# Preparing the maps of attention and of the experts between the feed-forward's slots, and splitting the first map's weights after the first gates

## The chip, the cores and the metric

The kernel runs on one core of one Trainium2 chip. The metric is the device time of one execution in microseconds (us), the lower the better; several executions are timed and their median is taken. A profiled execution gives for every instruction its engine, start and duration. The engines are PE (matrix multiplication; PEld are its weight loads), DVE (vector), ACT (activation), POOL (general) and SP, which here only issues DMAs. "Lnnn" in a line of the profile is a line of the kernel; L83 is a helper through which most operations pass.

## The reference

The input is x [4, 128, 64, 64], float32. Four layers follow, cut here to what the change touches:

```python
x = x + L0_conv_ref(gn(x))                    # layer 0: deformable convolution
x = g * x + x                                 # layer 1 ends with a gate g = sigmoid(conv(o) + b)
t = to_tokens(x)                              # [4, 4096, 128]

# layer 2, first half: products of cosines, then a feed-forward over 8 of 128 channels
def L2_attn_ref(x):
    a = x.reshape(B, S, 16, 8) + theta
    cp = cumprod(cos(a), axis=-1)
    x1 = layernorm(x + concat([cp[..., -1:], cp[..., 1:]]), gamma1, beta1)
    q = cos(phi) * cos(x1[..., :8])
    h = relu(q @ w1.T + b1)                   # 8 -> 2048
    return layernorm(x1 + h @ w2.T + b2, gamma2, beta2)
t = t + L2_attn_ref(ln(t))

# layer 2, second half, and layer 3, second half: eight experts, the best two of each token
def ffn_ref(x):
    p = softmax(x @ router_w + router_b); top_p, top_i = top_k(p, 2)
    e = einsum('bnd,edc->bnec', x, expert_w) + expert_b
    return sum over the two of top_p / sum(top_p) * e[top_i]
t = t + ffn_ref(ln(t))

# layer 3, first half: additive attention over the earlier tokens
def L3_attn_ref(x):
    f, g = x @ W1[:128], x @ W1[128:]         # 16 columns each
    score = tanh(f_i + g_j + b1) @ w2 + b2
    e = exp(score) * (j < i)
    return (e / (e.sum(j) + 1e-10)) @ x
t = t + L3_attn_ref(ln(t))
t = t + ffn_ref(ln(t))
```

## The kernel before

The whole activation stays in on-chip memory as one tile X of 128 partitions by 16,384 columns. The function at the end of the file calls the layers in turn: layer0, layer1, layer2, attention_maps, then for the experts of layer 2 moe_prepare and moe, then moe_prepare for layer 3, attention, and moe again.

**Order.** Most operations go through an object InOrder: each is pinned behind the one traced before it on the same engine. Operations issued with the plain engine object may be placed elsewhere on their engine by the scheduler. Memory is taken from pools that are opened and closed around a stage; PSUM, where PE writes, is handed out in tiles of 512 columns.

**layer2** works on 16 groups (p) of eight tiles of 128 tokens. It first loads the feed-forward's first weights by 16 DMAs on SP (L1522) and splits them into a leading and a remaining part with eight instructions (L1526 iota on POOL, to L1532 on DVE). The gates of layer 1 come next: gate(k) loads a block `oin` by SP, multiplies on PE into `psg`, takes the sigmoid on ACT into `g`, updates X on DVE, and two steps later transposes X on PE (`psf`) and copies it back on ACT. Four gates run ahead; the others stand between the slots of the first groups.

A loop over p from -3 to 16 and s from 0 to 7 calls slot(p, s). One slot issues on PE four matmuls `phh` of the next half group's hidden units (32 rows each, one buffer each, of a pool of four), then four matmuls for each of two sums `pff`, and between them the other stages of groups p+3 (A: first normalization, u, turns k, remainder a), p+2 (cosine, products on POOL in a_products, B: second normalization), p+1 and p-1 (D: third normalization; ptt transposes back, d_add adds it to x1, d_norm on ACT, d_sum with three POOL instructions adds to X). Of the four phh of a slot, DVE rectifies one or none (ON_VECTOR) and ACT the others into `hid`. The gates' psg and psf use the same four buffers (tag "phh").

**attention_maps** (L2056 to L2139) works out the small matrices of attention's approximation, hide, wf, wg, cw, sb, sw and tiny, from W1, w2 and the biases: three loads, an iota and shifts, some 30 small DVE instructions, transposes and matmuls through a PSUM tile `aux`.

**moe_load** and **moe_prepare** load the router and expert weights (`rw`, `ew`), subtract their last row from all rows (two matmuls by `last` into `pse`, L1834, and one into `psw`, L1838; the subtractions are L1836 and L1839), replace the last row by the biases with two DMAs on SP (L1840, L1841), clear `rws` (L1842) and copy the router's weights into it four times (L1844). moe then starts with an iota, `rank`, and the statistics of its first tiles (bn_stats into `w`).

**attention** starts with a memset of the eight tiles `v` on POOL, then statistics(0, 0): bn_stats of eight tiles into `st`, variance with seven POOL instructions, the root on ACT, the normalization into `v`, transposes `D`, the copy `vT`, and the factors F and G. SP writes X to memory (`kept`, L2161) at its start.

Of the kernel before, what the change touches and what calls it, by code (L numbers as in the profile page):

```python
# [27 lines left out]
NE = 8  # L28
# [61 lines left out]
class Kernel:  # L90
# [1400 lines left out]
    def layer2(self):  # L1491
# [8 lines left out]
        with ExitStack() as ctx:  # L1500
# [24 lines left out]
            nc.gpsimd.iota(half, pattern=[[0, 1]], base=0, channel_multiplier=1)  # L1525
            nc.vector.tensor_scalar(half, half, 4, 1, ALU.arith_shift_right, ALU.bitwise_and)  # L1526
            nc.vector.tensor_copy(parts[:, 1:2], half)
            nc.vector.tensor_scalar(parts[:, 0:1], parts[:, 1:2], -1.0, 1.0, ALU.mult, ALU.add)
            nc.vector.tensor_copy(w1b.bitcast(F32R), w1a)
            nc.vector.tensor_sub(w1a, w1a, w1b)  # L1530
            nc.vector.tensor_scalar(w1b, w1b, parts[:, 0:1], None, ALU.mult)
            nc.vector.scalar_tensor_tensor(w1T, w1a, parts[:, 1:2], w1b, ALU.mult, ALU.add)  # L1532
# [7 lines left out]
            V, S, G = nc.vector, nc.scalar, nc.gpsimd  # L1540

# [270 lines left out]
    def moe_load(self, ctx, layer):  # L1812
        cp = ctx.enter_context(self.tc.tile_pool(name=f"m{layer}w", bufs=1, side="right" if layer == 2 else None))
        rw = self.load(cp, f"router_w{layer}", [P, NE], eng=self.nc.sync)
        ew = self.load(cp, f"expert_w{layer}", [P, NE * P], eng=self.nc.sync)
        self.moe_maps[layer] = rw, ew

    def moe_prepare(self, ctx, layer):


        tc, nc = self.tc, self.nc
        LAST = P - 1
        rw, ew = self.moe_maps[layer]

        cp = ctx.enter_context(tc.tile_pool(name=f"m{layer}r", bufs=1))
        rws = cp.tile([P, 4, P], F32, name="rws")
        self.moe_maps[layer] = ew, rws
        with tc.tile_pool(name=f"m{layer}i", bufs=1) as ip, \
                tc.tile_pool(name=f"m{layer}j", bufs=1, space=PSUM) as pp:
            last = ip.tile([P, P], F32, name="last")  # L1830
            nc.vector.tensor_copy(last, self.ident[:, LAST:P].to_broadcast([P, P]))
            ps = pp.tile([P, NE * P], F32, name="pse")
            for h in range(2):
                nc.tensor.matmul(ps[:, 512 * h:512 * (h + 1)], last, ew[:, 512 * h:512 * (h + 1)],  # L1834
                                 start=True, stop=True)
            nc.vector.tensor_sub(ew, ew, ps)  # L1836
            ps = pp.tile([P, NE], F32, name="psw")
            nc.tensor.matmul(ps, last, rw, start=True, stop=True)  # L1838
            nc.vector.tensor_sub(rw, rw, ps)  # L1839
            nc.sync.dma_start(ew[LAST:P, :], self.ins[f"expert_b{layer}"].rearrange("e c -> (e c)").unsqueeze(0))  # L1840
            nc.sync.dma_start(rw[LAST:P, :], self.ins["rows"][ROW[f"router_b{layer}"]].unsqueeze(0))  # L1841
            nc.vector.memset(rws, 0.0)  # L1842
            for j in range(4):
                nc.vector.tensor_copy(rws[:, j, 32 * j:32 * j + NE], rw)  # L1844
# [211 lines left out]
    def attention_maps(self, ctx):  # L2056


        tc, nc = self.tc, self.nc
        LAST = P - 1  # L2060
        cp = ctx.enter_context(tc.tile_pool(name="r3k", bufs=1))
        with tc.tile_pool(name="r3a", bufs=2, space=PSUM) as aux, tc.tile_pool(name="r3w", bufs=1) as wp:
            w1f = self.load(wp, "att_w1f", [P, P])
            w1g = self.load(wp, "att_w1g", [P, P], view=self.ins["att_w1g"][:, 0, :])
            w2z = self.load(wp, "att_w2z", [P, 56])
            hide = cp.tile([P, P], F32, name="hide")
            nc.gpsimd.memset(hide, 0.0)
            nc.gpsimd.affine_select(out=hide, in_=hide, compare_op=ALU.is_gt, fill=1.0e4, base=0,
                                    pattern=[[1, P]], channel_multiplier=-1)
            wf = [cp.tile([P, P], F32, name=f"wf{b}") for b in range(2)]  # L2070
            wg = [cp.tile([P, P], F32, name=f"wg{b}") for b in range(2)]
            cw = [cp.tile([P, 1], F32, name=f"cw{b}") for b in range(2)]
            sb = cp.tile([P, 1], F32, name="sb")
            sw = cp.tile([P, 1], F32, name="sw")

            with tc.tile_pool(name="r3m", bufs=1) as mp:

                pi = mp.tile([P, 5], I32, name="pi")
                bits = mp.tile([P, 6], F32, name="bits")
                nc.gpsimd.iota(pi, pattern=[[0, 5]], base=0, channel_multiplier=1)  # L2080
                for k in range(5):
                    nc.vector.tensor_scalar(pi[:, k:k + 1], pi[:, k:k + 1], k, 1,
                                            ALU.arith_shift_right, ALU.bitwise_and)
                nc.vector.tensor_copy(bits[:, 0:5], pi)
                has = mp.tile([P, 2, 2, 16], F32, name="has")
                nc.vector.memset(has, 0.0)
                for b in range(2):
                    nc.vector.memset(bits[:, 5:6], float(b))
                    for hs, a0, a1 in ATT_SETS:
                        nc.vector.tensor_copy(has[hs, b, 0, a0:a1], bits[hs, 0:a1 - a0])  # L2090
                        nc.vector.tensor_scalar(has[hs, b, 1, a0:a1], bits[hs, 0:a1 - a0], -1.0, 1.0,
                                                ALU.mult, ALU.add)

                last = mp.tile([P, P], F32, name="last")
                nc.vector.tensor_copy(last, self.ident[:, LAST:P].to_broadcast([P, P]))
                wd = mp.tile([P, 2, 16], F32, name="wd")
                ps = aux.tile([P, 512], F32, name="aux")
                for k, w in enumerate((w1f, w1g)):
                    nc.tensor.matmul(ps[:, k * 16:(k + 1) * 16], last, w[:, 0:16], start=True, stop=True)
                    nc.vector.tensor_sub(wd[:, k, :], w[:, 0:16], ps[:, k * 16:(k + 1) * 16])  # L2100
                sel = mp.tile([16, 4, P], F32, name="sel")
                ps = aux.tile([P, 512], F32, name="aux")
                for k in range(4):
                    nc.tensor.transpose(ps[0:16, k * P:(k + 1) * P], has[:, k // 2, k % 2, :], self.ident)
                nc.vector.tensor_copy(sel.rearrange("p k c -> p (k c)"), ps[0:16, :])
                maps = mp.tile([16, 2, P], F32, name="maps")
                ps = aux.tile([P, 512], F32, name="aux")
                for k in range(2):
                    nc.tensor.transpose(ps[0:16, k * P:(k + 1) * P], wd[:, k, :], self.ident)
                nc.vector.tensor_copy(maps.rearrange("p k c -> p (k c)"), ps[0:16, 0:2 * P])  # L2110

                bl = mp.tile([16, P], F32, name="bl")
                nc.vector.memset(bl, 0.0)
                nc.vector.tensor_copy(bl[:, LAST:P], self.col("att_b1")[0:16, :])
                nc.vector.tensor_add(maps[:, 1, :], maps[:, 1, :], bl)

                w2 = w2z[0:16, 24:25]
                for b in range(2):
                    ps = aux.tile([P, 512], F32, name="aux")
                    for k, m in enumerate((wf, wg)):  # L2120
                        nc.tensor.matmul(ps[:, k * P:(k + 1) * P], maps[:, k, :], sel[:, 2 * b, :],
                                         start=True, stop=True)
                        nc.vector.tensor_copy(m[b], ps[:, k * P:(k + 1) * P])
                    nc.tensor.matmul(ps[:, 2 * P:2 * P + 1], sel[:, 2 * b + 1, :], w2, start=True, stop=True)
                    nc.vector.memset(cw[b], 1.0)
                    for hs in ((slice(32, 64),), (slice(32, 64), slice(64, 128)))[b]:
                        nc.vector.tensor_scalar(cw[b][hs, :], ps[hs, 2 * P:2 * P + 1], 2.0, None, ALU.mult)
# [501 lines left out]
def tile_conv_attn_hybrid(ctx: ExitStack, tc: tile.TileContext, ins: dict, out: bass.AP):  # L2629
# [10 lines left out]
    with two:  # L2640
        k.moe_prepare(two, 2)
        k.moe(2)
# [82 lines left out]
```

## Time and profile before

| what | us |
|---|---|
| median of three runs | 5165.38 |
| lowest and highest | 5161.37, 5171.79 |
| the profiled execution | 5169.17 |
| its span, first to last instruction | 5167.3 |
| granted clock of PE, mean | 0.931 |
| busy time of PE, DVE, ACT, POOL | 4526.2, 3699.5, 3592.7, 3255.3 |
| gates' first matmul psg | 1851.22 |
| first phh of the feed-forward | 1938.66 |
| end of its last pff | 2526.84 |
| first bn_stats of the experts, layer 2 | 2549.01 |
| last sum of the experts, layer 2, on X | 2867.66 |
| first bn_stats of attention | 2874.61 |

The lower six rows are points on the profiled execution's time axis, in us from the span's start. A line of the timeline reads: start, duration, engine, line of the kernel, operation, output<-input, sizes, how many follow one another, and in brackets how long the engine sat idle before it and what ended that. A line of the windows reads: stretch, its length, then busy time and number of instructions of each engine, then the clock granted to PE, the busy share of the DMA engines and the GB/s moved.

### The profile page before, as it was taken

How to read it: one execution, taken by the hardware profiler on the slowest of the kernel's cores; microseconds unless marked ns; L12 is line 12 of the kernel's file. 1: busy time of each engine (PE TensorE's matmuls, PEld its weight loads, DVE VectorE, ACT ScalarE, POOL GpSimd, SP SyncE). 2: the span in 40 equal slices, each digit the busy share in tenths (PEclk: the TensorE clock that was granted, in tenths of full speed). 3: DMA queues.
4: the chain of work that ended last, by engine and by line, in shares of the span. 5: the costliest groups of instructions: out<-in, count | busy, mean ns of one | idle time of the engine just before them, and what ended most of it. 6: DMA issues, size and time to landing. Idle time of an engine off the chain costs nothing. (4 is left out here: it accounts for less than half of the span.)

```text
span 5167.3 us, 65672 instructions
## 1 busy us (share of the span) xinstructions
PE 4526.2 (88%) x22430; PEld 2474.0 (48%) x22430; DVE 3699.5 (72%) x7376; ACT 3592.7 (70%) x5440; POOL 3255.3 (63%) x3073
## 2 busy tenths in 40 slices
PE   5776777668889959999799799999999999999798
PEld 3665666536556624444344344444444444444344
DVE  3889888768988658887477566676676666665675
ACT  3353534345565557777576699999999999999675
POOL 0627365415555525555279688888788888887488
PEclk7898988888888879999899899999999999999899
DMA  5556555300000030000000000000000000000000
GB/s 170 140 139 149 143 150 142 91 6 1 17 13 11 17 90 1 1 1 1 6 17 33 17 1 1 1 1 1 1 1 1 1 1 1 1 1 1 5 29 33
DMA packets 67239, 185.59 MB, mean 36 GB/s; under 512 B 13254, under 2 KB 16518, under 8 KB 65224
## 3 DMA queue, kind: packets, MB, share of 16 engines
q1 hardware_dynamic: 56856, 164.94, 10.9%
q0 software_dynamic: 6272, 12.86, 1.5%
q8 instruction: 181, 2.97, 0.2%
q10 hardware_dynamic: 3760, 3.43, 0.2%
q14 instruction: 170, 1.39, 0.1%
HBM read 131.83 MB, written 49.36 MB: 35 GB/s over the span
## 5 line engine op out<-in xcount | busy, mean ns | idle before, releaser
L83 POOL TENSOR_TENSOR r<-r 128x512 f32<-128x512 f32 (+1 forms) x1088 | 1348.7, 1241 | 335.8 <-DVE r L83 274.9
L83 DVE TENSOR_TENSOR r<-r,num 128x1024 f32<-128x1024 f32 (+1 forms) x1088 | 975.6, 928 | 601.9 <-PE num L83 503.6
L83 PE MATMUL D<-F,G 32*128 32x512 f32 (+3 forms) x4608 | 1145.1, 576 | 1.3 <-DVE den L83 0.9
L83 PE MATMUL num<-F,G 32*128 32x512 f32 (+3 forms) x4608 | 1057.9, 590 | 6.9 <-DVE r L83 4.0
L83 ACT ACTIVATE r<-r 128x2048 f32<-128x2048 f32 (+4 forms) x610 | 1018.5, 1679 | 52.0 <-POOL r L83 5.8
L83 ACT ACTIVATE r<-D 128x1536 f32<-128x1536 f32 (+1 forms) x544 | 763.3, 1403 | 54.4 <-PE D L83 31.4
L83 PEld LDWEIGHTS D<-F,G 32*128 32x128 f32 x4608 | 487.2, 185 | 372.9 <-issue 234.2
L83 PE MATMUL acc<-ident,pr 128*128 128x128 f32 x3200 | 449.0, 304 | 221.7 <-DVE pr L83 221.7
L83 PE MATMUL acc<-r,v 128*128 128x512 f32 (+3 forms) x1152 | 598.3, 606 | 0.7 <-ACT r L83 0.7
L83 POOL DMA_INDIRECT px<-tab,idx x196 | 385.8, 1968 | 255.9 <-DMA v<-tab 164.8
L83 PEld LDWEIGHTS acc<-ident,pr 128*128 128x128 f32 x3200 | 415.8, 159 | 261.7 <-DVE pr L83 252.8
L83 POOL TENSOR_TENSOR x<-x 128x512 f32<-128x512 f32 (+2 forms) x320 | 405.6, 1267 | 150.8 <-DVE x L83 84.6
L83 PEld LDWEIGHTS num<-F,G 32*128 32x128 f32 x4608 | 384.1, 184 | 225.9 <-issue 112.4
L83 PE MATMUL pff<-hid,w_ffn_w2T 128*128 128x512 f32 x1024 | 468.5, 601 | 0.0
L83 PE MATMUL pex<-w_expert_w,vT 128*128 128x512 f32 x1024 | 462.4, 600 | 1.6 <-DVE x L83 1.6
L83 DVE TENSOR_TENSOR pr<-v,wt 128x2560 f32<-128x2560 f32 x160 | 453.7, 2851 | 9.7 <-PE acc L83 9.7
L83 PEld LDWEIGHTS acc<-r,v 128*128 128x128 f32 x1152 | 174.3, 188 | 382.4 <-issue 186.4
L83 ACT ACTIVATE x<-pex,gate 128x128 f32<-128x128 f32 x896 | 256.6, 367 | 104.9 <-PE pex L83 77.8
L83 ACT ACTIVATE hid<-phh,cols 128x512 f32<-128x512 f32 x416 | 252.8, 688 | 68.1 <-PE phh L83 68.1
L83 PEld LDWEIGHTS pex<-w_expert_w,vT 128*128 128x128 f32 x1024 | 191.2, 193 | 216.4 <-issue 160.5
L83 PEld LDWEIGHTS pff<-hid,w_ffn_w2T 128*128 128x128 f32 x1024 | 185.3, 191 | 200.6 <-issue 200.6
L83 POOL TENSOR_TENSOR X<-X,sl 128x512 f32<-128x512 f32 x32 | 76.6, 2392 | 315.4 <-ACT sl L83 315.4
(501 smaller groups left out, 7633.6 us busy)
## 6 DMA issues: line engine op xcount, KB each, us to landing
v<-tab SPq DMA_DIRECT2D x320, 256.0 KB
oms<-omw SPq DMA_DIRECT2D x32, 432.0 KB
omr<-oms SPq DMA_DIRECT2D x32, 432.0 KB
X<-in_x_dram SPq DMA_DIRECT2D x8, 1024.0 KB
tab<-vb SPq DMA_DIRECT2D x64, 128.0 KB
o<-o SPq DMA_DIRECT2D x32, 256.0 KB
oin<-o SPq DMA_DIRECT2D x32, 256.0 KB
kept<-X SPq DMA_DIRECT2D x4, 2048.0 KB
```

Source lines behind the costliest of these rows:

```text
L83: return lambda *args, **kwargs: self.tc.keep_in_program_order(op(*args, **kwargs))
```

## The change

Five parts go together.

1. The split of the first weights leaves its place ahead of the gates. Its eight instructions become first_map(), which runs in three pieces after slots 0, 1 and 2 of p=-2, each pinned behind that slot's instructions on its engine. The 16 loads stay.
2. moe_prepare for both layers and attention_maps become generators. later_maps() chains them, and one step runs after each slot from p=1 on: 37 steps, up to slot 4 of p=5. Their PSUM tiles come from bank(), which takes one of the four buffers of phh. A step either fills a bank on PE or reads it on DVE, not both.
3. The weights' and maps' places are taken before layer2 (moe_space, attention_space), and the weights are loaded by SP after the last slot of p=-1 (moe_fetch). The biases' loads are issued by SP in steps of their own.
4. In attention, the memset of `v` moves from POOL to DVE, the two instructions for `tiny` are issued there, and the variance of the first two groups runs on DVE instead of POOL.
5. The calls of attention_maps and moe_prepare between the stages are gone.

```diff
@@ layer2
-            nc.gpsimd.iota(half, pattern=[[0, 1]], base=0, channel_multiplier=1)
-            nc.vector.tensor_scalar(half, half, 4, 1, ALU.arith_shift_right, ALU.bitwise_and)
-            nc.vector.tensor_copy(parts[:, 1:2], half)
-            nc.vector.tensor_scalar(parts[:, 0:1], parts[:, 1:2], -1.0, 1.0, ALU.mult, ALU.add)
-            nc.vector.tensor_copy(w1b.bitcast(F32R), w1a)
-            nc.vector.tensor_sub(w1a, w1a, w1b)
-            nc.vector.tensor_scalar(w1b, w1b, parts[:, 0:1], None, ALU.mult)
-            nc.vector.scalar_tensor_tensor(w1T, w1a, parts[:, 1:2], w1b, ALU.mult, ALU.add)
...
+            def first_map():
+                G.iota(half, pattern=[[0, 1]], base=0, channel_multiplier=1)
+                V.tensor_scalar(half, half, 4, 1, ALU.arith_shift_right, ALU.bitwise_and)
+                V.tensor_copy(parts[:, 1:2], half)
+                V.tensor_scalar(parts[:, 0:1], parts[:, 1:2], -1.0, 1.0, ALU.mult, ALU.add)
+                yield
+                V.tensor_copy(w1b.bitcast(F32R), w1a)
+                V.tensor_sub(w1a, w1a, w1b)
+                yield
+                V.tensor_scalar(w1b, w1b, parts[:, 0:1], None, ALU.mult)
+                V.scalar_tensor_tensor(w1T, w1a, parts[:, 1:2], w1b, ALU.mult, ALU.add)
+                yield
+
+            def later_maps():
+                def bank():
+                    return ph.tile([P, 512], F32, name="phm", tag="phh")
+                mp = ctx.enter_context(tc.tile_pool(name="l2m", bufs=1))
+                last = mp.tile([P, P], F32, name="last")
+                V.tensor_copy(last, self.ident[:, P - 1:P].to_broadcast([P, P]))
+                for layer in (2, 3):
+                    yield from self.moe_prepare(nc, layer, last, bank)
+                yield from self.attention_maps(nc, mp, last, bank)
...
+            begun, beside = first_map(), later_maps()
             for p in range(-3, NG + 1):
                 for s in range(8):
                     slot(p, s)
                     for _ in range(GATES[s] if p < -1 else LAST_GATES[s] if p < 0 else 0):
                         gate(next(steps))
+                    if p == -2:
+                        next(begun, None)
+                    if p == -1 and s == 7:
+                        for layer in (2, 3):
+                            self.moe_fetch(layer)
+                    if p >= 1:
+                        next(beside, None)
...
+    def moe_fetch(self, layer):
+        rw, ew, _ = self.moe_maps[layer]
+        self.nc.sync.dma_start(rw, self.ins[f"router_w{layer}"])
+        self.nc.sync.dma_start(ew, self.ins[f"expert_w{layer}"])
+
+    def moe_prepare(self, nc, layer, last, bank):
...
+        for h in range(2):
+            hs = slice(512 * h, 512 * (h + 1))
+            ps = bank()
+            nc.tensor.matmul(ps, last, ew[:, hs], start=True, stop=True)
+            yield
+            nc.vector.tensor_sub(ew[:, hs], ew[:, hs], ps)
+            yield
+        ps = bank()
+        nc.tensor.matmul(ps[:, 0:NE], last, rw, start=True, stop=True)
+        yield
+        nc.vector.tensor_sub(rw, rw, ps[:, 0:NE])
+        nc.vector.memset(rws, 0.0)
+        yield
+        self.nc.sync.dma_start(ew[LAST:P, :], self.ins[f"expert_b{layer}"].rearrange("e c -> (e c)").unsqueeze(0))
+        self.nc.sync.dma_start(rw[LAST:P, :], self.ins["rows"][ROW[f"router_b{layer}"]].unsqueeze(0))
+        for _ in range(3):
+            yield
+        for j in range(4):
+            nc.vector.tensor_copy(rws[:, j, 32 * j:32 * j + NE], rw)
+        yield
...
@@ attention_maps, one of its pairs of steps
+        sel = mp.tile([16, 4, P], F32, name="sel")
+        ps = bank()
+        for k in range(4):
+            nc.tensor.transpose(ps[0:16, k * P:(k + 1) * P], has[:, k // 2, k % 2, :], self.ident)
+        yield
+        nc.vector.tensor_copy(sel.rearrange("p k c -> p (k c)"), ps[0:16, :])
+        yield
...
@@ attention
-                    nc.gpsimd.memset(v[:, :, LAST:P], 1.0)
+                    nc.vector.memset(v[:, :, LAST:P], 1.0)
+                tc.keep_in_program_order(nc.scalar.activation(tiny, sb, AF.Exp, scale=-1.0))
+                nc.vector.tensor_scalar(tiny, tiny, self.ident[:, LAST:P], 1e-10, ALU.mult, ALU.mult)
...
-                def variance(n, q):
+                def variance(n, q, on=None):
...
-                    variance(n, q)
+                    variance(n, q, nc.vector)
...
@@ the order of the layers
         k.layer1(gate)
-        k.moe_load(two, 2)
+        k.attention_space(ctx)
+        k.moe_space(ctx, 3)
+        k.moe_space(two, 2)
         k.layer2()
-    k.attention_maps(ctx)
-    k.moe_load(ctx, 3)
     with two:
-        k.moe_prepare(two, 2)
         k.moe(2)
-    k.moe_prepare(ctx, 3)
     k.attention()
     k.moe(3)
```

More of the change, by code (lines that the diff above doesn't have):

```diff
@@ L1808, in layer2 @@
                         gate(next(steps))
[L1812 to L1821, printed above, removed]
+                    if p == -2:
+                        next(begun, None)
@@ new lines, in layer2, with moe_space @@
+                    if p == -1 and s == 7:
[3 more added lines that the diff above has]
+                        next(beside, None)
+            assert next(beside, beside) is beside
+    def moe_space(self, ctx, layer):
+        cp = ctx.enter_context(self.tc.tile_pool(name=f"m{layer}w", bufs=1, side="right"))
+        rw = cp.tile([P, NE], F32, name=f"w_router_w{layer}")
+        ew = cp.tile([P, NE * P], F32, name=f"w_expert_w{layer}")
+        self.moe_maps[layer] = rw, ew, cp.tile([P, 4, P], F32, name="rws")
@@ L1822, in moe_prepare @@
+    def moe_fetch(self, layer):
[3 more added lines that the diff above has]
+    def moe_prepare(self, nc, layer, last, bank):
         LAST = P - 1
-        rw, ew = self.moe_maps[layer]
-        cp = ctx.enter_context(tc.tile_pool(name=f"m{layer}r", bufs=1))
-        rws = cp.tile([P, 4, P], F32, name="rws")
+        rw, ew, rws = self.moe_maps[layer]
         self.moe_maps[layer] = ew, rws
[L1828 to L1844, printed above, removed]
@@ L2052, in moe @@
                     flip(q)
-    def attention_maps(self, ctx):
-        tc, nc = self.tc, self.nc
-        LAST = P - 1
[L2061 to L2127, printed above, removed]
-                ps = aux.tile([P, 512], F32, name="aux")
-                nc.tensor.matmul(ps[:, 0:1], self.ones[0:16, :], w2, start=True, stop=True)
-                nc.vector.tensor_add(sb, ps[:, 0:1], self.row("att_b2"))
-                size = mp.tile([16, 1], F32, name="size")
-                nc.scalar.activation(size, w2, AF.Abs)
-                nc.tensor.matmul(ps[:, 2:3], self.ones[0:16, :], size, start=True, stop=True)
-                nc.vector.tensor_copy(sw, ps[:, 2:3])
-            tiny = cp.tile([P, 1], F32, name="tiny")
-            nc.scalar.activation(tiny, sb, AF.Exp, scale=-1.0)
-            nc.vector.tensor_scalar(tiny, tiny, self.ident[:, LAST:P], 1e-10, ALU.mult, ALU.mult)
-        self.att_maps = hide, wf, wg, cw, sb, sw, tiny
@@ new lines, in attention_space @@
+    def attention_space(self, ctx):
+        cp = ctx.enter_context(self.tc.tile_pool(name="r3k", bufs=1, side="right"))
+        self.att_maps = (cp.tile([P, P], F32, name="hide"), [cp.tile([P, P], F32, name=f"wf{b}") for b in range(2)],
+                         [cp.tile([P, P], F32, name=f"wg{b}") for b in range(2)],
+                         [cp.tile([P, 1], F32, name=f"cw{b}") for b in range(2)],
+                         cp.tile([P, 1], F32, name="sb"), cp.tile([P, 1], F32, name="sw"),
+                         cp.tile([P, 1], F32, name="tiny"))
@@ new lines, in attention_maps @@
+    def attention_maps(self, nc, mp, last, bank):
+        plain = self.nc
+        LAST = P - 1
+        hide, wf, wg, cw, sb, sw, _ = self.att_maps
+        w1f = self.load(mp, "att_w1f", [P, P], eng=plain.sync)
+        w1g = self.load(mp, "att_w1g", [P, P], view=self.ins["att_w1g"][:, 0, :], eng=plain.sync)
+        w2z = self.load(mp, "att_w2z", [P, 56], eng=plain.sync)
+        nc.gpsimd.memset(hide, 0.0)
+        nc.gpsimd.affine_select(out=hide, in_=hide, compare_op=ALU.is_gt, fill=1.0e4, base=0,
+                                pattern=[[1, P]], channel_multiplier=-1)
+        pi = mp.tile([P, 5], I32, name="pi")
+        bits = mp.tile([P, 6], F32, name="bits")
+        nc.gpsimd.iota(pi, pattern=[[0, 5]], base=0, channel_multiplier=1)
+        yield
+        for k in range(5):
+            nc.vector.tensor_scalar(pi[:, k:k + 1], pi[:, k:k + 1], k, 1,
+                                    ALU.arith_shift_right, ALU.bitwise_and)
+        nc.vector.tensor_copy(bits[:, 0:5], pi)
+        has = mp.tile([P, 2, 2, 16], F32, name="has")
+        nc.vector.memset(has, 0.0)
+        yield
+        for b in range(2):
+            nc.vector.memset(bits[:, 5:6], float(b))
+            for hs, a0, a1 in ATT_SETS:
+                nc.vector.tensor_copy(has[hs, b, 0, a0:a1], bits[hs, 0:a1 - a0])
+                nc.vector.tensor_scalar(has[hs, b, 1, a0:a1], bits[hs, 0:a1 - a0], -1.0, 1.0,
+                                        ALU.mult, ALU.add)
+            yield
+        wd = mp.tile([P, 2, 16], F32, name="wd")
+        ps = bank()
+        for k, w in enumerate((w1f, w1g)):
+            nc.tensor.matmul(ps[:, k * 16:(k + 1) * 16], last, w[:, 0:16], start=True, stop=True)
+        yield
+        for k, w in enumerate((w1f, w1g)):
+            nc.vector.tensor_sub(wd[:, k, :], w[:, 0:16], ps[:, k * 16:(k + 1) * 16])
+        yield
+        sel = mp.tile([16, 4, P], F32, name="sel")
+        ps = bank()
+        for k in range(4):
+            nc.tensor.transpose(ps[0:16, k * P:(k + 1) * P], has[:, k // 2, k % 2, :], self.ident)
+        yield
+        nc.vector.tensor_copy(sel.rearrange("p k c -> p (k c)"), ps[0:16, :])
+        yield
+        maps = mp.tile([16, 2, P], F32, name="maps")
+        ps = bank()
+        for k in range(2):
+            nc.tensor.transpose(ps[0:16, k * P:(k + 1) * P], wd[:, k, :], self.ident)
+        yield
+        nc.vector.tensor_copy(maps.rearrange("p k c -> p (k c)"), ps[0:16, 0:2 * P])
+        bl = mp.tile([16, P], F32, name="bl")
+        nc.vector.memset(bl, 0.0)
+        nc.vector.tensor_copy(bl[:, LAST:P], self.col("att_b1")[0:16, :])
+        nc.vector.tensor_add(maps[:, 1, :], maps[:, 1, :], bl)
+        yield
+        w2 = w2z[0:16, 24:25]
+        for b in range(2):
+            ps = bank()
+            for k, m in enumerate((wf, wg)):
+                nc.tensor.matmul(ps[:, k * P:(k + 1) * P], maps[:, k, :], sel[:, 2 * b, :],
+                                 start=True, stop=True)
+            nc.tensor.matmul(ps[:, 2 * P:2 * P + 1], sel[:, 2 * b + 1, :], w2, start=True, stop=True)
+            yield
+            for k, m in enumerate((wf, wg)):
+                nc.vector.tensor_copy(m[b], ps[:, k * P:(k + 1) * P])
+            nc.vector.memset(cw[b], 1.0)
+            for hs in ((slice(32, 64),), (slice(32, 64), slice(64, 128)))[b]:
+                nc.vector.tensor_scalar(cw[b][hs, :], ps[hs, 2 * P:2 * P + 1], 2.0, None, ALU.mult)
+            yield
+        size = mp.tile([16, 1], F32, name="size")
+        nc.scalar.activation(size, w2, AF.Abs)
+        yield
+        ps = bank()
+        nc.tensor.matmul(ps[:, 0:1], self.ones[0:16, :], w2, start=True, stop=True)
+        nc.tensor.matmul(ps[:, 2:3], self.ones[0:16, :], size, start=True, stop=True)
+        yield
+        nc.vector.tensor_add(sb, ps[:, 0:1], self.row("att_b2"))
+        nc.vector.tensor_copy(sw, ps[:, 2:3])
+        yield
@@ L2222, in moments @@
                         nc.vector.bn_stats(st[0][:, k, :], T[:, n * NT + 4 * q + k, :])
-                def variance(n, q):
-                    s = st[0]
+                def variance(n, q, on=None):
+                    s, on = st[0], on or nc.gpsimd
                     mean = sp.tile([P, 8], F32, name="mean")
@@ L2229, in variance @@
                     d = sp.tile([P, 8], F32, name="d")
-                    nc.gpsimd.tensor_tensor(mean, s[:, :, 1], s[:, :, 4], ALU.add)
-                    nc.gpsimd.tensor_scalar(mean, mean, 0.5, None, ALU.mult)
-                    nc.gpsimd.tensor_tensor(d, s[:, :, 1], s[:, :, 4], ALU.subtract)
-                    nc.gpsimd.tensor_tensor(d, d, d, ALU.mult)
-                    nc.gpsimd.tensor_scalar(d, d, 32.0, None, ALU.mult)
-                    nc.gpsimd.tensor_tensor(rstd, s[:, :, 2], s[:, :, 5], ALU.add)
-                    nc.gpsimd.tensor_tensor(rstd, d, rstd, ALU.add)
+                    on.tensor_tensor(mean, s[:, :, 1], s[:, :, 4], ALU.add)
+                    on.tensor_scalar(mean, mean, 0.5, None, ALU.mult)
+                    on.tensor_tensor(d, s[:, :, 1], s[:, :, 4], ALU.subtract)
+                    on.tensor_tensor(d, d, d, ALU.mult)
+                    on.tensor_scalar(d, d, 32.0, None, ALU.mult)
+                    on.tensor_tensor(rstd, s[:, :, 2], s[:, :, 5], ALU.add)
+                    on.tensor_tensor(rstd, d, rstd, ALU.add)
                     norm[n, q] = mean, rstd
```

## The prediction

> **What bounds the kernel now.** I read the share of each engine first, then the windows of the feed-forward stage (the FFN), then the timeline at the three places that the change empties: ahead of the gates, between the FFN and the experts of layer 2, and between those and attention.
>
> ```profile
> PE 4526.2 (88%) x22430; PEld 2474.0 (48%) x22430; DVE 3699.5 (72%) x7376; ACT 3592.7 (70%) x5440; POOL 3255.3 (63%) x3073
> 1976.00:2013.00 37.00, 37.00 (x125) 15.88 (x124) 29.94 (x83) 28.93 (x52) 17.88 (x14) 1.00 0.00 1
> 2200.00:2237.00 37.00, 35.60 (x110) 14.85 (x109) 30.83 (x82) 27.34 (x49) 20.53 (x16) 1.00 0.00 1
> ```
> The columns of a window are its length, then the busy time of PE, PEld, DVE, ACT and POOL, and the granted clock. Over the span PE leads, but the share says nothing of a place. In the FFN PE is busy 37.00 of 37 at p=1 and 35.60 later: whatever is put there lands on the engine that sets the end.
>
> ```profile
> 2003.52 0.51 PE L83 MATMUL phh<-qT,w_ffn_w1T 32*128 32x512 f32 x4
> 2003.96 2.41 PE L83 MATMUL pff<-hid,w_ffn_w2T 128*128 128x512 f32 x5
> 2004.05 1.84 ACT L83 ACTIVATE hid<-phh,cols 128x512 f32<-128x512 f32 x3 [0.52 <-PE phh L83]
> 2091.05 0.50 PE L83 MATMUL phh<-qT,w_ffn_w1T 32*128 32x512 f32 x1
> 2092.77 0.51 PE L83 MATMUL phh<-qT,w_ffn_w1T 32*128 32x512 f32 x3 [1.22 <-DVE hid L83]
> 2101.30 2.17 PE L83 MATMUL phh<-qT,w_ffn_w1T 32*128 32x512 f32 x4
> ```
> A free slot issues its four phh together in 0.51 us. From p=2 on a period takes about 37.5 us (s=0 at 2011.65 and, two later, at 2086.60) against 34.1 at p=1 (1977.53 to 2011.65), and PE loses 1.22 in s=1 and 1.66 (2.17-0.51) in s=3 to hid that come late, some 2.9 a period. DVE works without a gap in s=6 to 3 and idles 5.3 in s=3 to 6.
>
> **Ahead of the gates.**
> ```profile
> 1849.22 0.43 DVE L1529 CAST w1s<-w1s 128x512 fp32r<-128x512 f32 x1 [16.42 <-DMA w1s<-in_ffn_w1T_dram]
> 1851.22 5.46 PE L83 MATMUL psg<-oin,w_conv_w 128*128 128x512 f32 x6 [18.81 <-DVE w1s L1531]
> 1886.27 2.34 POOL L83 TENSOR_TENSOR u<-u,a 128x1024 f32<-128x1024 f32 x1
> 1888.64 0.87 DVE L83 BATCH_NORM_STATS2 stB<-u 128x6 f32<-128x128 f32 x4 [4.23 <-POOL u L83]
> ```
> PE's first gate is put down to L1531, which ends at 1850.90; but the gates' own input is loading until about 1850.5 on the same queue. Taking the split away gives 0 (input as late) to 1.4 us; I take 1.0. Its eight instructions reappear after three slots of p=-2, in order. There the iota stands on POOL behind a_products, whose last instruction ends at 1888.61, and DVE's first instruction waits for it; queued behind that on DVE are variance A (done at 1881.83 before) and an X (1883.68), and behind those the gates and stB. DVE used the 4.23 us before stB's start for nothing else, so 6 small instructions (0.95), an X (0.73), cast and sub (1.12), ts and stt (1.24) and the half's three (0.9) now follow 1888.6: 4.9 us, and variance B ends near 1896.8 instead of 1891.86. The table load, gates, u, and at last the FFN's first phh (1938.66) hang on it. Bounds: 0 if the slack of the gates takes it all, 5.5 if nothing does. I take 4.9-1.0 = **+3.9**.
>
> **The FFN.** 37 steps run after the slots from p=1 on. Twelve of them open a bank: one of the four buffers that phh uses, read on DVE one step later, after the whole next slot's instructions. That slot's fourth phh must wait until ACT has emptied the first: ACT starts 0.53 after phh (2003.52 to 2004.05), needs 0.69 and a wake of about 0.05, and only then may pff follow: 1.70 after the slot's start instead of 0.43 (2003.96-2003.52). So 1.27 us where PE sets the pace, twelve times: 15.2. The added matmuls are those that stand at the boundaries now, at the full clock 1.96+0.28 for a layer (layer 3's, below 2860), and about 3 for attention's: 7.5. DVE's share is near 12 us (two L1836 of 1.22, two memsets of 0.48, the others 0.06 to 0.72 each). Not all of it adds up: in s=1 and s=3 PE waits 2.9 us a period already, so banks in slots 0 to 3 and 7 may hide there, while DVE's work counts; at s=4 to 6 DVE idles and PE counts in full. By group: layer 2's steps at p=1, with no stall to hide in, three banks 3.8, PE 2.2, DVE 0.9; layer 3's at p=2 and 3 4.2; attention's seven-instruction steps 1.5, its banks at p=4 4.7 and at p=5 4.5: 22. Bounds: 10, if only the four banks in slots 4 and 5 (5.1) and two thirds of PE's 7.5 count; 28, if all banks, all PE work and 5 of DVE's do. I take **+20**: nearer the upper end, since p=1 shows a full PE, and below the 22 for what the stalls take.
> The two bias loads on SP, the three weight loads and POOL's three instructions (0.20, 0.13, 0.29) cost nothing: SP issues nothing else there and POOL is at 20.53 of 37; were POOL full they would cost 0.6.
> Some DVE instructions stretch while POOL works: k<-k took 0.69 us at the fastest and 2.37 in the median of 16. The Trainium skill (SBUF — State Buffer, "Who interferes with whom") says why: VectorE's two-port forms and two-input forms share a port pair with GpSimd under an exclusive lock, so that the later one blocks fully. This speaks against the change, as the rws, has and bits steps are copies. By that rule ten steps would wait about half a POOL instruction of 2.2 each, five eighths of them on DVE's busy stretch, an estimate of 7 more: FFN +27 instead of +20.
>
> **Between FFN and experts.**
> ```profile
> 2526.88 0.69 ACT L83 ACTIVATE ff<-pff,cols 128x512 f32<-128x512 f32 x1 [3.71 <-PE pff L83]
> 2530.01 0.40 DVE L2082 TENSOR_SCALAR pi<-pi 128x1 int32<-128x1 int32 x5 [2.60 <-POOL pi L2080]
> 2531.15 0.69 DVE L83 TENSOR_TENSOR x<-x,ptt 128x512 f32<-128x512 f32 x1
> 2536.92 3.18 ACT L83 ACTIVATE u<-x,meanD,rstdD 128x128 f32<-128x128 f32 x8 [1.73 <-DVE meanD L83]
> 2540.19 4.08 POOL L83 TENSOR_TENSOR u<-u,rows 128x1024 f32<-128x1024 f32 x2 [9.94 <-ACT u L83]
> 2549.01 2.65 DVE L83 BATCH_NORM_STATS2 w<-X 128x6 f32<-128x128 f32 x8
> ```
> ptt ends at 2528.28, yet x<-x,ptt runs at 2531.15, behind the maps' pi. Without them: x 2528.35, stD 2529.1, variance (six at 0.17) to 2531.0, root 0.30, the two small ones, u at 2531.9, POOL's three (6.5) from 2535.1 to 2541.6, memset, iota, rank 0.6: bn_stats at 2542.2 instead of 2549.01. What is late next is POOL's last sum, which the maps never touched. **-6.8**; 5 if rank's chain stays longer, 8 if the experts' first sums need not wait for POOL.
>
> **Between experts and attention.**
> ```profile
> 2866.94 0.72 POOL L83 TENSOR_TENSOR X<-X,x 128x256 f32<-128x256 f32 x1
> 2868.45 0.25 SPq L1841 DMA_DIRECT2D w_router_w<-in_rows_dram  x1
> 2874.31 0.39 DVE L1844 COPY rws<-w_router_w 128x8 f32<-128x8 f32 x4 [13.30 <-DMA w_router_w<-in_rows_dram]
> 2874.61 1.64 DVE L83 BATCH_NORM_STATS2 st<-X 128x6 f32<-128x128 f32 x8
> ```
> The bias load, queued on SP behind kept<-X, holds DVE until 2874.31. Without it bn_stats needs X and a place for st; st's pool lies where the experts' x stood, which POOL reads until 2867.66. Gain 6.9 (14.9 if only the tile x under it counts, last read at 2859.6). Variance on DVE costs 0.4 less in the first group, and 1.45 more in the second, where seven instructions of 0.17 now stand ahead of the vT copy (2889.53) that PE waits 3.21 for: **-5.8**, bounds -13.9 and -5.
>
> **The sum.** 3.9+20-6.8-5.8 = +11.3. The profiled execution took 5169.17 (span 5167.3 and 1.9 around it): 5180.5. It stands 3.8 above the median of the three runs, so on the median 5176.7, say 5177.
>
> **The rivals.**
> 1. The steps hide. PE's stalls, 2.9 a period over p=2 to 5, are 11.6 us, and DVE's idle 5.3 a period is 21: all steps from p=2 on run in them, only p=1's three banks, 3.8, are left, and the sum is 3.9+3.8-6.8-5.8 = -4.9: 5160.5, and with the gates' chain at nothing 5156.6. For it: that idle time. Against: four banks fall in s=4 and 5, where PE doesn't wait. It decides under an FFN growth of 8.7, where the sum changes sign.
> 2. Attention starts at the release of one x, at 2859.7: 11.3-8.1 = +3.2, 5169. For it: X's other tiles are done by then. Against: the memset of `has` at 2526.92 waited for the whole stage's PSUM and SBUF to fall free, so places go back as pools.
> 3. Heavier: DVE's busy stretch delays each read of a bank, so that half of the twelve are held a second slot, 6 by 1.27. FFN +28: sum +19.3, 5185. For it: hid already come late by DVE (the 1.22). Against: DVE idles in s=3 to 6, so a delay is made good within a period.
>
> **How the numbers follow.** My forecast has 0.44, the first rival 0.27, the second 0.13, the third 0.16. About 0.2% (10.3 us) either way can't be told from no change here: 5155.1 to 5175.7. The forecast's own range with the FFN at 15 to 25 is 5172 to 5182: slower 0.28, same 0.16. The first rival ends under 5155 where the gates lose nothing or attention gains more than 5.8: faster 0.14, same 0.13. The second: faster 0.04 (with the FFN near its lower bound), same 0.08, slower 0.01. The third: slower 0.16. Together faster 0.18, same 0.37, slower 0.45. The range, 5156 to 5190, reaches from the first rival with all its gains to the third with the gates and attention at their worse bounds and 3 more.
>
> **What would show it.** The half's first instruction on DVE near 1888.7 and the first phh near 1942.5, not 1938.66. From first phh to last pff 608 instead of 588.2. In slots after a bank's step the fourth phh waits 1.2 for ACT's hid. bn_stats of the experts 15.4 after the last pff (2526.84 before, 22.2), attention's first right behind POOL's last X. Wrong I am if the FFN grows by less than 10, or if a boundary keeps a wait that I took for the maps': another load, or X itself.

## The result, and the profile after

Ten runs of the changed kernel have a median of 5186.39 us (5176.15 to 5199.68), ten of the kernel before 5165.99 us (5157.95 to 5178.83). The ratio is 1.0042, with a 95% interval of 1.0028 to 1.0056: the changed kernel is slower by some 20 us.

The profiled execution took 5199.68 us, 13 above its median, and it issues the gates' first load, ahead of the first edit, 7.3 us later than the profile before (1854.80 and 1847.50). So stages are compared below, not points in time.

| stage | before | after | difference |
|---|---|---|---|
| gates' first load (oin, on SP) to first phh | 91.16 | 95.02 | +3.9 |
| first phh to the end of the last pff (the FFN) | 588.18 | 625.79 | +37.6 |
| to the first bn_stats of the experts, layer 2 | 22.18 | 14.95 | -7.2 |
| to the last sum on X by these experts | 318.64 | 317.00 | -1.6 |
| to attention's first bn_stats | 6.95 | 0.03 | -6.9 |
| to attention's first matmul of D by F and G | 18.19 | 19.81 | +1.6 |
| to the first bn_stats of the experts, layer 3 | 1929.98 | 1923.75 | -6.2 |
| to the end | 344.53 | 346.04 | +1.5 |

The boundaries went as forecast. The FFN lost nearly twice what was forecast. First the boundaries, from the timeline after: ahead of the FFN, between the FFN and the experts, and ahead of attention.

```profile
1893.32 2.34 POOL L83 TENSOR_TENSOR u<-u,a 128x1024 f32<-128x1024 f32 x1
1895.77 0.15 DVE L83 TENSOR_SCALAR half<-half 128x1 int32<-128x1 int32 x1 [7.53 <-POOL half L83]
1896.22 0.16 DVE L83 TENSOR_TENSOR meanA<-stA 128x8 f32<-128x8 f32 x1
1898.72 0.86 DVE L83 BATCH_NORM_STATS2 stB<-u 128x6 f32<-128x128 f32 x4
...
2575.64 0.69 ACT L83 ACTIVATE ff<-pff,cols 128x512 f32<-128x512 f32 x1 [3.71 <-PE pff L83]
2577.07 0.69 DVE L83 TENSOR_TENSOR x<-x,ptt 128x512 f32<-128x512 f32 x1 [6.95 <-PE ptt L83]
2583.76 4.07 POOL L83 TENSOR_TENSOR u<-u,rows 128x1024 f32<-128x1024 f32 x2 [5.26 <-ACT u L83]
2590.55 1.64 DVE L83 BATCH_NORM_STATS2 w<-X 128x6 f32<-128x128 f32 x5
...
2906.83 0.72 POOL L83 TENSOR_TENSOR X<-X,x 128x256 f32<-128x256 f32 x1
2907.58 1.64 DVE L83 BATCH_NORM_STATS2 st<-X 128x6 f32<-128x128 f32 x8 [9.37 <-POOL X L83]
2923.36 0.68 DVE L83 COPY vT<-acc 128x512 f32<-128x512 f32 x1
```
DVE idles 7.53 us for the iota behind a_products, with variance A queued behind it. x<-x,ptt runs 1.5 after the last pff (4.3 before), and now POOL's sum on X comes last. Attention's bn_stats starts 0.03 after POOL's last X.

Now the FFN after: the engines' shares of the whole span, the windows of p=1, of p=5 and of a period without steps, and then the way from s=6 of p=2 to s=0 of p=3.

```profile
PE 4546.2 (87%) x22430; PEld 2485.4 (48%) x22430; DVE 3704.1 (71%) x7398; ACT 3594.2 (69%) x5439; POOL 3247.0 (62%) x3051
```
```profile
1985.00:2029.00 44.00, 39.56 (x119) 17.10 (x118) 29.06 (x87) 28.03 (x49) 12.49 (x13) 0.96 0.00 1
2159.00:2206.00 47.00, 39.73 (x129) 18.11 (x128) 32.05 (x94) 28.34 (x50) 20.12 (x16) 0.96 0.00 1
2243.00:2281.00 38.00, 36.59 (x114) 15.31 (x112) 31.80 (x82) 28.35 (x51) 21.53 (x16) 1.00 0.00 1
```
```profile
2069.58 0.28 PE L83 MATMUL phm<-w_router_w,last 128*128 128x8 f32 x2
2069.79 0.51 PE L83 MATMUL phh<-qT,w_ffn_w1T 32*128 32x512 f32 x3
2071.12 0.50 PE L83 MATMUL phh<-qT,w_ffn_w1T 32*128 32x512 f32 x1 [0.82 <-ACT hid L83]
...
2075.18 0.50 PE L83 MATMUL phh<-qT,w_ffn_w1T 32*128 32x512 f32 x3
2075.80 2.33 DVE L83 TENSOR_SCALAR q8k<-x 128x64 f32<-128x64 f32 x1
2078.80 0.15 DVE L83 TENSOR_TENSOR w_router_w<-w_router_w,phm 128x8 f32<-128x8 f32 x1
2079.01 0.79 PE L83 MATMUL phh<-qT,w_ffn_w1T 32*128 32x512 f32 x1 [3.33 <-DVE w_router_w L83]
2080.63 5.77 PE L83 MATMUL pff<-hid,w_ffn_w2T 128*128 128x512 f32 x8
```
Over the span PE is busy 20 us more than before, and DVE 5; in the windows PE is idle for 4.4 us of p=1 (44.00-39.56) and 7.3 of p=5, though it gained work there. The bank is filled at 2069.58. In the next slot three phh go at once and the fourth waits for ACT, as forecast: 2071.12 instead of 2069.79. But DVE reads the bank only at 2078.80, since it is behind PE there, so in the slot after that the fourth phh finds no buffer either and waits 3.33 us for the read. One bank has then cost two slots, and the slot from 2075.18 to the next phh at 2086.33 takes 11.2 us instead of 4.5. Five of the twelve banks are held into a second slot in this way: PE waits 1.61, 3.33, 0.53, 4.21 and 0.66 us for their reads.

The wait is not all of it. In that slot eight pff take 5.77 us, where eight took 3.70 in the slot before. The same 1024 pff, before and after:

```profile
L83 PE MATMUL pff<-hid,w_ffn_w2T 128*128 128x512 f32 x1024 | 468.5, 601 | 0.0
L83 PE MATMUL pff<-hid,w_ffn_w2T 128*128 128x512 f32 x1024 | 476.4, 609 | 0.0
```
```profile
1938.66:2526.84 588.18, 570.44 (x1785) 242.83 (x1784) 443.99 (x1152) 432.22 (x759) 295.31 (x213) 0.99 0.00 1
1949.82:2575.61 625.79, 589.99 (x1823) 253.47 (x1822) 452.89 (x1208) 434.37 (x760) 292.58 (x216) 0.98 0.00 1
```
The first number behind the bar is the busy time in us. Over the FFN PE is idle 35.8 us instead of 17.7, which is 18.1 of the 37.6, and the pff are busy 7.9 longer; the added matmuls and the other matmuls share the last 11.6. The section on the hardware shows where the pff slow down.

### The profile page after: what moved, and what is told of

It reads as the page before. It is cut to its first block, busy times and chain, and to the rows that moved or that the text cites. A ratio compares the mean times of both kernels' runs of the same rounds, so it can differ in the third digit from the quotient of the medians.

```text
span 5197.2 us, 65671 instructions
## 1 busy us (share of the span) xinstructions
PE 4546.2 (87%) x22430; PEld 2485.4 (48%) x22430; DVE 3704.1 (71%) x7398; ACT 3594.2 (69%) x5439; POOL 3247.0 (62%) x3051
## 3 DMA queue, kind: packets, MB, share of 16 engines
q8 instruction: 181, 2.97, 0.2%
## 5 line engine op out<-in xcount | busy, mean ns | idle before, releaser
L83 DVE TENSOR_TENSOR pr<-v,wt 128x2560 f32<-128x2560 f32 x160 | 453.5, 2849 | 11.2 <-PE acc L83 11.2
```

What stands on the lines that cost most here:

```text
L83: return lambda *args, **kwargs: self.tc.keep_in_program_order(op(*args, **kwargs))
```

## The experiments

Two theories of the FFN's 37.6 us were set against each other: A, a bank lent from phh's four is held until DVE, late, has read it; B, the added DVE instructions lengthen DVE's busy stretch. The periods below are counted from the phh issued in s=7 of the period before, and the FFN from the first phh to the end of the last pff. All are from one profile of each kernel; the periods 6 to 12 of all kernels that do nothing there lie between 37.43 and 37.50 us. The last column is the median of the whole, with the number of runs; in the session of the early, late and bankless kernels one run of the kernel before took 5173.98.

| kernel | p=1 | p=2 | p=3 | p=4 | p=5 | FFN | whole (runs) |
|---|---|---|---|---|---|---|---|
| before | 34.12 | 37.46 | 37.48 | 37.48 | 37.46 | 588.18 | 5167.66 (13) |
| after | 43.98 | 40.66 | 42.41 | 47.28 | 46.76 | 625.79 | 5186.39 (10) |
| banks from pff | 35.94 | 38.43 | 41.00 | 42.68 | 38.81 | 600.46 | 5162.41 (1) |
| banks alone, at the change's places | 42.59 | 41.09 | 42.05 | 43.87 | 45.82 | 618.92 | 5200.09 (1) |
| banks alone, early | 36.20 | 39.56 | 39.57 | 39.56 | 39.57 | 612.92 | 5202.31 (1) |
| banks alone, late | 34.94 | 42.03 | 42.87 | 41.99 | 43.07 | 645.20 | 5235.03 (1) |
| bankless steps alone | 34.11 | 37.45 | 37.45 | 41.75 | 37.47 | 591.71 | 5166.57 (1) |
| split ahead | 42.37 | 40.66 | 42.63 | 47.28 | 46.79 | 623.50 | 5185.94 (1) |
| placed | 34.96 | 37.48 | 37.99 | 37.48 | 38.00 | 591.90 | 5151.65 (10) |

**Banks from pff's buffers instead of phh's.**
```diff
-                    return ph.tile([P, 512], F32, name="phm", tag="phh")
+                    return pf.tile([P, 512], F32, name="phm", tag="pff")
```


> The changed kernel, but each step's PSUM bank is one of the two buffers of pff instead of one of the four of phh; all steps stay where they are. Theory A (held banks: a bank lent from phh is given back only when DVE, late, has read it, and the next slot's fourth phh waits for that): the feed-forward, first phh to last pff, falls from 625.8 us to 600 to 610, and the slots of 11 us at s=0 to under 7. Theory B (DVE's time: the added DVE instructions, stretched by POOL, lengthen DVE's busy stretch): it stays at 618 or more.

The FFN took 600.46 us, the low end of A: 25.3 of the 37.6 went with the held buffers of phh. One run took 5162.41 us. A had expected every slot of 11 us to fall under 7; two did not: s=0 of p=4, behind the bankless steps, took 11.75, and s=0 of p=3 11.36. At p=3 the timeline of this kernel shows the same wait in another place:

```profile
2047.97 0.28 PE L83 MATMUL phm<-w_router_w,last 128*128 128x8 f32 x2
2057.48 0.15 DVE L83 TENSOR_TENSOR w_router_w<-w_router_w,phm 128x8 f32<-128x8 f32 x1
2057.69 2.93 PE L83 MATMUL pff<-hid,w_ffn_w2T 128*128 128x512 f32 x3 [4.35 <-DVE w_router_w L83]
```
Now pff of s=0 needs the buffer that DVE, late, hasn't read. That a bank is read late costs whichever pool it is from, once the pool's next tile is due.

**Twelve idle banks in the kernel before, at the change's places.**
```diff
+                    if held:
+                        V.tensor_copy(seen, held.pop()[:, 0:1])
+                    if (p, s) in BANKS:
+                        ps = ph.tile([P, 512], F32, name="phm", tag="phh")
+                        nc.tensor.matmul(ps, self.ident, w2T[:, 0:4, :].rearrange("p a b -> p (a b)"),
+                                         start=True, stop=True)
+                        held.append(ps)
```


> The kernel before, to which only twelve idle banks are added, at the same twelve places: each is one of phh's four buffers, filled by one matmul over 512 columns (1.02 us) and read one slot later by one DVE copy of a single column; the maps are prepared between the stages as before. Theory A: the feed-forward grows from 588.2 us to 610 to 625, with slots of 9 us or more where a bank is read after s=7. Theory B: only PE's 12 us, less what its stalls hide: 592 to 602.

618.92 us: +30.7 for banks whose reads are one column each, so DVE gets nearly no work. At most 12.2 of it is the fill (12 by 1.02; the change's own are shorter, 8.5 in all). For the banks it is A, not B. The slots at s=0 of p=3 and p=5 took 10.93 and 11.50.

**The same twelve, one a period, at two places.** Only the list of places differs: after s=3 of p=1 to 12 (read after s=4), or after s=6 (read after s=7).
```diff
+            BANKS = [(g, 3) for g in range(1, 13)]
```


> The kernel before with twelve idle banks of phh added, one in each period from p=1 to 12, filled after s=3 and read after s=4, where DVE isn't behind PE. Theory A (a held bank costs until DVE reads it, so its price goes by how far DVE is behind there): each costs the 1.27 us of the prediction and at most its fill of 1.02: the feed-forward 603 to 616 us instead of 588 to 589. Theory D (a bank costs the same wherever it is read): as e2's twelve, 30 us: 618 or more.

> As the early banks, twelve, one in each period from p=1 to 12, but filled after s=6 and read after s=7, where DVE is some 5 us behind PE. Theory A: the fourth phh of the next s=0 waits for DVE, 4 us or more a bank, and the feed-forward ends at 640 or more; slots of 9 us or more at s=0. Theory D: the same as the early ones within 5 us.

Early, the FFN took 612.92, 24.7 more: 2.06 a bank, about half of it the fill of 1.02 and half the wait. Late, with `BANKS` at (g, 6), it took 645.20, 57.0 more: 4.75 a bank. The price goes by the place, as A says. The timelines, early and then late:

```profile
2080.29 1.02 PE L83 MATMUL phm<-w_ffn_w2T,ident 128*128 128x512 f32 x2
2081.24 0.50 PE L83 MATMUL phh<-qT,w_ffn_w1T 32*128 32x512 f32 x3
2082.51 0.49 PE L83 MATMUL phh<-qT,w_ffn_w1T 32*128 32x512 f32 x1 [0.77 <-ACT hid L83]
```
```profile
2151.50 0.49 PE L83 MATMUL phh<-qT,w_ffn_w1T 32*128 32x512 f32 x1 [0.84 <-ACT hid L83]
2158.73 0.15 DVE L83 COPY seen<-phm 128x1 f32<-128x1 f32 x1
2159.02 0.76 PE L83 MATMUL phh<-qT,w_ffn_w1T 32*128 32x512 f32 x1 [2.97 <-DVE seen L83]
2160.62 6.07 PE L83 MATMUL pff<-hid,w_ffn_w2T 128*128 128x512 f32 x8
```
Early there is the one wait for ACT: the fourth phh starts 1.27 us after the first three, 2081.24 to 2082.51. Late there are both, and the pff that follow are slow too: the 1024 pff are busy 486.3 us with the late banks and 468.5 with the early ones, so 17.8 of the 57.0 are slower pff.

**The bankless steps alone, in the kernel before.**
```diff
+                    if p == 3 and s == 5:
...
+                        V.tensor_copy(bits[:, 0:5], pi)
+                        V.memset(has, 0.0)
+                    if p == 3 and s in (6, 7):
...
+                            V.tensor_copy(has[hs, b, 0, a0:a1], bits[hs, 0:a1 - a0])
```


> The kernel before with only the three bankless steps of attention's maps added (17 small DVE instructions and two of clearing, pi, bits and has, after slots 5, 6 and 7 of p=3, in the order of the change), on tiles of their own. Theory B for this one place (DVE's instructions ahead of a late hid): the slot s=0 of p=4 takes 9 us or more and the feed-forward grows by 5 to 8 us. Theory A alone: no more than 2.

The slot at s=0 of p=4 took 11.13 us, as B said; the FFN grew by 3.5, under B's 5 and over A's 2. For these three steps B holds, with a smaller size: p=4 lost 4.3, and the slots after s=0 lost less than usual (4.46 for 6.15 in s=1, where PE would have waited anyway). In the timeline of this kernel:

```profile
2081.82 0.50 PE L83 MATMUL phh<-qT,w_ffn_w1T 32*128 32x512 f32 x1
2082.38 2.34 POOL L83 TENSOR_TENSOR X<-X,u 128x1024 f32<-128x1024 f32 x1
2082.41 2.33 DVE L83 COPY has<-bits 32x5 f32<-32x5 f32 x1
2085.09 0.75 DVE L83 TENSOR_SCALAR hid<-phh,cols 128x512 f32<-128x512 f32 x1
2085.90 0.80 PE L83 MATMUL phh<-qT,w_ffn_w1T 32*128 32x512 f32 x3 [3.57 <-DVE hid L83]
...
2089.40 0.16 DVE L83 COPY has<-bits 32x5 f32<-32x5 f32 x1
```
The copy of 5 columns takes 2.33 us beside POOL's sum on X and 0.16 without it; hid stands behind it on DVE, and PE waits 3.57 for hid. These three steps are the only ones that were run alone.

**The split back ahead of the gates.** The eight instructions return to their old place in the changed kernel.


> The changed kernel with the first weights' split put back ahead of the gates; nothing else. If the split behind the first gates costs what the prediction said, the way from the gates' first load to the first phh falls from 95.0 us to 91 and the rest stays: about 4 us less in all. If the first phh is late for another reason it stays at 95.

From the gates' first load to the first phh 89.93 us instead of 95.02, the FFN 623.50; one run took 5185.94, which alone can't show 4 us in the whole. Over all kernels profiled here the way is 94.3 with the split behind the first gates (95.02, 93.61) and 88.6 to 91.2 with it ahead (seven kernels, mean 89.4): the move costs 4.9 us.

**Placed.** Split ahead, banks from pff, one bank a period filled after s=0 and read after s=3, the other steps after s=3 or 4, variance of attention's second group on POOL.
```diff
+            AT = (((0, 4),),
+                  ((1, 0), (1, 3), (2, 0), (2, 3), (3, 0), (3, 3), (3, 4), (4, 4)),
+                  ((4, 0), (4, 3), (5, 0), (5, 3), (6, 0), (6, 3), (6, 4), (7, 4)),
+                  ((1, 4), (2, 4), (5, 4), (7, 3), (8, 0), (8, 3), (9, 0), (9, 3), (10, 0), (10, 3),
+                   (11, 0), (11, 3), (12, 0), (12, 3), (12, 4), (13, 0), (13, 3)))
...
+                    for at, maps in zip(AT, todo):
+                        if (p, s) in at:
+                            next(maps)
```


> The changed kernel with the split ahead of the gates, banks from pff's two buffers, one bank in each period: filled after s=0, where PE waits anyway in s=1, read after s=3, where DVE idles; the steps without a bank after s=3 or 4; variance of attention's second group back on POOL. Theory A and theory B: the feed-forward at 588 to 593 us, since neither a phh buffer is held nor DVE's busy stretch lengthened; the gains between the stages stay (7.2 and 6.9), so the whole is 10 to 15 us under the kernel before. If PE's added 7.5 us alone cost (theory C), the feed-forward ends at 596 and the whole 5 us under before.

The FFN took 591.90 us, the boundaries 14.96 and 0.03, and D by F and G came 17.47 after bn_stats. Ten runs have a median of 5151.65 us against 5167.66 in 13 of the kernel before, 16 less and a little more than was expected; the ratio is 0.9969, interval 0.9955 to 0.9982. It is faster than both kernels, and the same steps cost the FFN 3.7 us, not 37.6, though DVE is busy 463.0 us of this FFN and 452.9 of the change's. Pool and places were changed together here: phh's buffers at these places were not tried.

```profile
2133.21 1.02 PE L83 MATMUL phm<-w_expert_w,last 128*128 128x512 f32 x2
2134.16 0.50 PE L83 MATMUL phh<-qT,w_ffn_w1T 32*128 32x512 f32 x1
2135.53 0.50 PE L83 MATMUL phh<-qT,w_ffn_w1T 32*128 32x512 f32 x3 [0.87 <-DVE hid L83]
2147.53 0.68 DVE L83 TENSOR_TENSOR w_expert_w<-w_expert_w,phm 128x512 f32<-128x512 f32 x1
```
The fill, at s=0 of p=5, stands where PE waited for hid before: the wait is 0.87 instead of 1.2, and the two slots s=0 and s=1 together take 11.1 us instead of 10.6.

## Why the prediction was right, and where it wasn't

The direction and the range held: forecast 5177 (5156 to 5190), measured 5186.39. That the range held is partly luck. The steps that the sum names measure +3.9, +37.6, -7.2 and -6.9+1.6 in the two profiles, +29.0 together against the forecast's +11.3; on the median before that is 5195, above the range. Stages that no step names gave 6.3 back (-1.6, -6.2 and +1.5), and the 2.3 that are left to the medians' 20.4 are less than single executions scatter. By its steps:

- **Ahead of the gates**, +3.9. The chain behind the iota was forecast at 4.9 and is 4.9 over nine kernels; the profile before has the longest way of its seven, so that the +3.9 of the two profiles meets the forecast by chance. The 1.0 that the split's removal should give isn't there: from the gates' load to psg it is 3.0 to 3.7 us with the split and 3.2 to 3.3 without it, so the load seems to set it.
- **The FFN**, +20, bounds 10 to 28: the step that failed, by size, at 37.6, outside its bounds. It took 1.27 us for each bank wherever it lay, and even let slots 0 to 3 and 7 hide theirs. The 1.27 is right where DVE keeps up (the early banks). Where the prediction itself had DVE busy without a gap, from s=6 to s=3, the read can come late, and the bank is missing in a second slot; read after s=7, a bank costs 4.75. Slots that it thought cheap held the dearest banks. The sum also has its matmuls at the full clock and no term for a slower one: the 1024 pff alone were busy 7.9 us longer. Of the 37.6, 25.3 went with phh's buffers; of the other 12.3, p=3 with its late pff bank has 3.5, and p=4 has 5.2, of which the bankless steps alone make 4.3; the last 3.6 lie in the other periods and weren't taken apart.
- **Stretched DVE instructions.** The Trainium skill (SBUF — State Buffer, "Who interferes with whom") has the later of two blocked fully; the copy at 2.33 beside 0.16 agrees. In the change four of the added DVE instructions were long (1.77, 1.05, 2.33 and 1.54 us), not ten steps; the first three stand ahead of s=0 of p=4, where the bankless steps cost 4.3 us alone.
- **Between FFN and experts**, -6.8: measured -7.2, and POOL's sum on X is what comes last, as said.
- **Ahead of attention**, -6.9 for the start and +1.05 for variance: -6.9 and +1.6. With the second group's variance on POOL the placed kernel has 17.47 where the change has 19.81.
- **The rivals.** Hidden steps: not in the change, but nearly so in the placed kernel, so the idle time it counted on is there; the change doesn't put the steps in it. Attention from 2859.7: no, it starts with POOL's last sum. Heavier: its mechanism, a bank held a second slot, is what happened, to five banks where it named six. It priced each at 1.27, 7.6 together; the five waits are 10.3, and the slower pff come on top.

## What to carry to other kernels

Whoever lends a buffer of a full pipeline's pool should ask when the reader's engine will really get to it, not in which slot the read is written: a pool of four for four tiles a slot has no spare, and a late reader costs twice. Put fills where the filling engine waits already, reads where the reading engine idles, and take the bank from the pool whose next tile is due last. Work that seems to fit by the sum of idle time can still be dear if it stands in order ahead of the one instruction that another engine waits for.

## What the runs showed of the hardware

**PE's pauses slow what follows.** In the kernel before, whose FFN has steady waits of 1.2 and 1.7 us a period, the granted clock is 1.00 from p=1 to the FFN's end. A pause of 3.33 in the change, and of 2.97 with the late banks, did not leave it so; the windows after these two pauses, of the change and then of the late banks:

```profile
2080.00:2087.00 7.00, 7.00 (x18) 3.18 (x18) 1.68 (x10) 4.56 (x6) 2.55 (x6) 0.64 0.00 1
2087.00:2092.00 5.00, 5.00 (x18) 2.27 (x17) 4.83 (x13) 2.56 (x6) 3.44 (x4) 1.00 0.00 0
```
```profile
2160.00:2167.00 7.00, 7.00 (x16) 3.03 (x14) 1.09 (x6) 4.41 (x5) 2.56 (x6) 0.60 0.00 0
2286.40:2293.40 7.00, 7.00 (x25) 3.42 (x26) 4.04 (x14) 6.14 (x8) 1.76 (x4) 1.00 0.02 4
```
The mean clock is 0.64 and 0.60 over 7 us, and eight pff take 5.77 and 6.07 instead of 3.70: about 2 us on top of the wait. The Trainium skill (TensorE: Matmul & The Clock Gate, "What's actually happening") has the clock halved after an idle window of about 3.4 us. Here the length of the pause alone doesn't decide. Of the twelve pauses of some 2.97 us with the late banks, four have a mean clock of 0.53 to 0.60 over the 7 us behind them and seven 0.76; behind the one left, the last line above, it is 1.00. In the placed kernel a pause of 1.36 us, at 2248.25, has 0.50 behind it:

```profile
2250.00:2253.40 3.40, 3.40 (x10) 1.92 (x8) 3.31 (x13) 2.19 (x5) 2.87 (x8) 0.50 0.00 0
```

**Attention's first 30 us.** From the first D by F and G to the experts of layer 3 the kernel before took 1929.98 and the change 1923.75, which no step had forecast. The windows that hold the first matmuls, before, after and in the placed kernel:

```profile
2893.00:2906.00 13.00, 13.00 (x43) 5.99 (x44) 3.85 (x11) 7.54 (x8) 1.57 (x1) 0.53 0.00 1
```
```profile
2927.00:2935.00 8.00, 7.48 (x36) 3.46 (x38) 1.48 (x3) 5.54 (x6) 0.97 (x1) 0.93 0.00 0
```
```profile
2885.00:2893.00 8.00, 7.48 (x44) 3.86 (x44) 4.19 (x12) 7.18 (x9) 1.58 (x1) 1.00 0.00 0
```
The clock came back later in the kernel before. The five kernels with the old boundary took 1929.98, 1929.67 (early banks), 1927.45 (banks at the change's places), 1924.86 (bankless steps) and 1924.19 (late banks): with the same code from the FFN's end on, the clock comes back at one time or another. The four with the new boundary all took 1923.75 to 1924.30. So it stays open whether these 6 us are chance or whether the new boundary helps the clock to come back early; what decides it wasn't tried.
